# Loads by urgency in a planned four-block kernel: SyncE's time in the orders, first loads on two queues, a bias row behind its buffer

## The chip, the cores and the metric

The kernel runs on one core of a Trainium2 chip. The metric is the device time of one execution in microseconds (us), and the number compared is the median of several runs. A core has five engines, each with its own instruction queue: TensorE (PE; its weight loads are PEld), VectorE (DVE), ScalarE (ACT), GpSimd (POOL) and SyncE (SP), which here only issues transfers from HBM. An engine takes its queue strictly in order: an instruction that waits holds everything behind it.

## What is computed

The reference takes x and a context, both 8 x 128 x 256 in float32, and passes x through four transformer blocks, L0 to L3. All attend to the context.

```
x = L0(x, ctx)   # LN; q from x, k and v from ctx; 16 heads of 16; key mask; LN; MLP 256-1024-256
x = L1(ctx, x)   # keys from ctx and x together; key mask; RMS norm; MLP
x = L2(x, ctx)   # two cross-attentions of 16 heads of 128, each with one learned key and value; MLP
x = L3(x, ctx)   # self-attention with a score mask, cross-attention with a score mask; MLP
```

In L2 the value path has two bias vectors, bv (of the projection) and bias_v (the learned value). The kernel needs their difference as a row of 512 numbers, repeated over all 128 partitions, for each group of four heads.

## The kernel before, in words

**Tiling.** The 8 sequences are split into four threads of two (SIZES), 256 tokens each. `blocks(T)` (L1351) walks a thread through L0 to L3. Threads 0 and 1 start at once; thread 2 starts when thread 0 has left L1 (`front_done`), thread 3 when thread 1 has and thread 0 has left L2 (`wide_done`). Each thread loads its own copy of all weights into eleven slots of 512 KB (NWT), at most four for one thread (NW); `loader(T)` does this. Thread 0 alone makes keys and values of two L2 groups ahead of everything else (AHEAD, 'l10' and 'l11'), so that TensorE has work while L0's chain is short of it.

**The order of the work** is not written out: a planner makes it while the program is built. `Plan` is a simulation of the five engines in Python. Coroutines (`attention`, `mlp`, `group`, `softmax`, ...) ask for an instruction on an engine with `op(eng, f)`; when an engine is free in the simulation, `_choose` takes the request with the smallest urgency (U for the kind of work, plus LATE for the thread and block), runs f, which emits the instruction, and holds the engine for the time that `_weight` gives. `either` lets ScalarE or VectorE take a piece, whichever is free first. If TensorE has nothing to do and `Clock` thinks that its clock is about to be halved, `idle_work` emits a filler, one product of the identity with itself (mm<-ident). The result is one fixed queue for each engine. On the chip only the queues and the semaphores count: where the planner's times are wrong, an instruction stands in the wrong place and its engine waits.

**Loads.** `dma` (L408) asks for SP, then counts 2.8 ns for each KB and 1900 ns to landing. An issue holds SP for 60 ns in the plan (`op`, L341). Nearly all loads ask with urgency 0. The first are x, cols (all per-partition biases, 109 KB) and ctxT (the context's slice) of each thread, from `inputs()`.

**The bias rows.** `value_bias` (L1282) waits for one of two bv slots, loads bv and bb (bias_v) and has GpSimd subtract bb from bv. The pool has two bv buffers but one bb buffer; the plan knows nothing of the latter, so a bb load may be put in SyncE's queue while GpSimd has not yet read the last one. `keys_values` makes the bv tile before it spawns this. The value products (`values`, then `take` on VectorE: vw<-mm,bv) need the row.

**In the profile** every compute instruction has line L329, where `Engine` calls it, and every load L415; so instructions are told apart by tile names: mm, tl and sc are PSUM banks, w a weight, hT a transposed normed input, kb keys, queries or hidden parts, vw values, k, q, v the small attentions' operands, mp their maxima, t scores, pt transposed probabilities, at and attnT attention outputs, xn a normed x, row an output bias.

Of the kernel before, what the change touches and what calls it, by code (L numbers as in the profile page):

```python
# [14 lines left out]
AF = mybir.ActivationFunctionType  # L15
ALU = mybir.AluOpType
AX = mybir.AxisListType

P = 128
# [6 lines left out]
NW, NWT = 4, 11  # L26
# [34 lines left out]

WARM = True
AHEAD = [[(1, 0), (1, 1)], [], [], []]
U = {'take': 0.33, 'taken': -1, 'norm': 0.36, 'mask': 1.35, 'k': 2.41, 'q': 1.92, 'v': 2.5, 'by key': 0.5, 'softmax': 2.4, 'weights': 0.74, 'pairs': 0.3, 'out': 0.94, 'mlp norm': 0.75, 'mlp 1': 3.6, 'mlp 2': 2.28, 'wide norm': -1, 'wide k': 3.49, 'wide q': 4.0, 'wide v': 4.5, 'wide s': 1.19, 'wide': -0.42, 'ahead': 2.48}
LATE = [(2.3, -0.18, 0.84, -0.88, 1.83, -0.17, 2.53, 1.2, 3.66, 1.59), (7.76, 6.61, 5.49, 5.66, 1.7, 0.2, 4.52, 3.1, 7.31, 7.88), (1.86, 2.79, 2.79, -0.1, 2.14, -1, 4.58, 4.78, 5.62, 1.93), (0.03, 1.63, -0.02, 0.92, 0.05, 2.99, -1, 0.16, -1, -1)]


class Event:
# [14 lines left out]
class Plan:  # L83
# [28 lines left out]
    def spawn(self, gen, urgency, after=0):  # L112
        end = Event()
        self.live[id(gen)] = gen
        self._later(self.now + after, (gen, urgency, end), None)
        return end
# [68 lines left out]
        return start + self.weight  # L185

    def run(self):
        self.now = max(self.until.values())
        while self.events or self.asked:
            while self.events and self.events[0][0] <= self.now:  # L190
                _, _, proc, value = heapq.heappop(self.events)
                self._step(proc, value)
            for eng in self.until:
                if self.until[eng] <= self.now:
                    got = self._choose(eng)
                    if not got and eng == "PE" and self.idle_work and (self.events or self.asked):
                        self.weight = 0
                        if self.clock.lazy(self.now) and self.idle_work():
                            self.until[eng] = self._end(eng)
                            self.log.append((eng, self.now, self.until[eng] - self.now, "idle", 2))  # L200
                    if got:
                        _, a, (_, ns, f, lat, table), load = got
                        self.asked.remove(a)
                        self.weight, self.shared, self.wrote, self.count = ns, False, [], 0
                        if load:
                            self.weight += 1295
                            self.table = table[0]
                        value = f()
                        end = self._end(eng)
                        self.until[eng] = end  # L210
                        self.log.append((eng, self.now, end - self.now, f.__qualname__.replace("four_blocks.<locals>.", "").replace("<locals>.", ""), self.count))
                        self._later(end + (self.SEEN[eng] if lat is None else lat), a[2], value)
            at = [self.events[0][0]] if self.events else []
            at += [t for t in self.until.values() if t > self.now]
            if not at:
                break
            self.now = max(self.now, min(at))
        stuck = []
        for g in self.live.values():
            while g:  # L220
                stuck.append(f"{g.gi_code.co_name}:{g.gi_frame.f_lineno}")
                g = g.gi_yieldfrom
        assert not stuck, f"waits without end: {stuck}"


class Clock:


    W, LITTLE, MUCH = 3413, 0.48, 0.87

    def __init__(self):
        self.t, self.busy, self.fast = 0.0, 0.0, False
# [3 lines left out]
    def lazy(self, now):  # L236

        self._go(now, False)
        self.spans = [(a, b) for a, b in self.spans if b > now - self.W]
        return not self.fast or sum(b - max(a, now - self.W) for a, b in self.spans) < 0.55 * self.W  # L240

    def _go(self, to, busy):
        while self.t < to:
# [19 lines left out]
def _weight(eng, name, args, kw):  # L263

    aps = [x for x in (*args, *kw.values()) if isinstance(x, bass.AP)]
    sizes = [x.free_size() for x in aps]
    n = max(sizes)
    by_part = sum(m == 1 for m in sizes[1:]) if n > 2 else max(0, len(aps) - 2) if name == "tensor_scalar" else 0
    on_sbuf = all(x.space == bass.MemoryType.SB for x in aps)
    if eng == "PE":  # L270
# [9 lines left out]
    if eng == "ACT":  # L280
        if "accum_out" in kw:
            return 385, False
        if name == "copy":
            return 61 + 0.824 * n, False
        return 127 + 0.805 * n + (40 if isinstance(kw.get("bias"), bass.AP) else 0) + (
            90 if isinstance(kw.get("scale"), bass.AP) else 0), False
    if eng == "DVE":
        if name == "reciprocal":
            return 65 + 6.25 * n, False
        if name in ("bn_stats", "bn_aggr"):  # L290
            return (325 if name == "bn_stats" else 99), False
        if n <= 8:
            return 68, False
        if name in ("tensor_scalar", "tensor_copy") and on_sbuf:
            return 75 + 0.8 * n + 55 * by_part, True
        two = name in ("tensor_tensor", "scalar_tensor_tensor") and sum(
            x.space == bass.MemoryType.SB and x.free_size() > 1 for x in aps[1:]) == 2
        return 72 + 1.03 * n + 55 * by_part, two
# [40 lines left out]


def op(eng, f, lat=None, table=None):  # L341
    return ((eng, 60 if eng == "SP" else 0, f, lat, table),)


EXP = ("exp",)
# [5 lines left out]
def four_blocks(ctx: ExitStack, tc: tile.TileContext, a: dict, out: bass.AP):  # L351
# [33 lines left out]
    pt_small, pt_wide, tm_slots = Slots(2), Slots(2), Slots(2)  # L385
    kb_slots, v_slots = Slots(20), Slots(4)
    attn_lock, x1_slots = Slots(2), Slots(2)
    row_slots, bv_slots, w_slots = Slots(2), Slots(2), Slots(NWT)

    def kb():  # L390
        return new(act, [P, 2 * P], "kb", bufs=20)
# [13 lines left out]
        at = COL_AT[name] + k  # L405
        return cols[:, at : at + n]

    def dma(f, kb_):  # L408

        yield op("SP", f)  # L410
        plan.dma_until = max(plan.dma_until, plan.now) + kb_ * 2.8
        yield plan.dma_until - plan.now + 1900

    def load(dst, src, kb_):
        return dma(lambda: nc.sync.dma_start(out=dst, in_=src), kb_)  # L415

    ident = new(const, [P, P], "ident")
    make_identity(tc.nc, ident)
# [86 lines left out]
    def loader(T):  # L505
        names = list(weight_list())
        first = {f"l{i}{hg}{x}" for i, hg in AHEAD[T.h] for x in "kv"}
        ahead = [x for x in names if x[0] in first]
        names = [x for x in names if x[0] not in first]
        for name, shape, pieces in names[:2] + ahead + names[2:]:  # L510
            yield (T.w_slots, 1)
            yield (w_slots, 1)
            t = T.w[name] = new(wpool, shape, "w", bufs=NWT)
            ends = [spawn(load(at(t), src, int(np.prod(shape)) // 256 // len(pieces)), 0) for at, src in pieces]
            T.w_in.setdefault(name, Event())
            spawn(all_then(ends, T.w_in[name]), 0)

# [32 lines left out]
    def asks(r):  # L550
        yield r
# [613 lines left out]
    def keys_values(T, i, hg, step_back):  # L1165

        n = f"l{i}{hg}"
        ks, vs = [], []
        bv = new(wpool, [P, 512], "bv", bufs=2)
        bv_in = spawn(value_bias(bv, i, hg), U["mask"] + step_back)  # L1170
        nb, nt = T.nb, T.nt
        v_in = [Event() for _ in range(nb)]

# [22 lines left out]
        def values():  # L1196
# [3 lines left out]
            for b in range(nb):  # L1200
# [9 lines left out]
                        )  # L1210

                def take(p, b=b, t=t):
                    yield op("DVE", lambda: nc.vector.tensor_tensor(t, p, bv, ALU.add))
                    plan.set(v_in[b])
                yield from product([f], take)
            drop(T)
# [62 lines left out]
            yield e  # L1279
        drop(T)  # L1280

    def value_bias(bv, i, hg):  # L1282
        s = slice(hg * 512, (hg + 1) * 512)
        yield (bv_slots, 1)
        bb = new(wpool, [P, 512], "bb", bufs=1)
        e = spawn(load(bv, a[f"L2_bv{i}"][:, s].partition_broadcast(P), 256), 0)
        yield from load(bb, a[f"L2_bias_v{i}"][:, s].partition_broadcast(P), 256)
        yield e
        yield op("POOL", lambda: nc.gpsimd.tensor_tensor(bv, bv, bb, ALU.subtract))

    def after_scores(T, i, hg, b, s, vs, v_in, n):
        t = new(act, [P, 516], "t", bufs=NT_).rearrange("p (h k) -> p h k", h=4)
# [111 lines left out]
    def inputs():  # L1404
        for T in threads:
            h = T.h
            if h == 0:
                first = new(const, [P, 1], "first")
                spawn(asks(op("ACT", lambda: nc.scalar.activation(first, ident[:, :1], AF.Exp), None, EXP)), 0)
            e = spawn(load(T.x, a["x"][T.batches].rearrange("b p d -> p b d"), 128 * T.nb), 0)  # L1410
            spawn(all_then([e], T.ready), 0)
            if h == 0:
                e = spawn(load(cols, a["cols"], 140), 0)
                spawn(all_then([e], cols_in), 0)
            e = spawn(load(T.ctx, a["ctxT"].rearrange("(c p) t -> p c t", p=P)[:, :, T.tokens], 128 * T.nb), 0)
            spawn(all_then([e], ctx_in[h]), 0)
            spawn(blocks(T), 0)
            yield 2000 if h == 0 else 8000
    plan.idle_work = idle_work if WARM else None
    spawn(inputs(), 0)  # L1420
    spawn(learned_keys(), 5.0)
# [43 lines left out]
```

## Time and profile before

| what | value |
|---|---|
| runs | 1213.44, 1214.82, 1214.67 us; median 1214.67 |
| profiled execution | 1218.14 us, its span 1216.3 us, granted TensorE clock 0.986 |
| instructions | 21992 |
| TensorE weight loads (PEld) busy | 950.5 us (78%) |
| ACT_TABLE_LOAD (the switch between exp and gelu) | 42, 53.9 us |
| DMA moved | 145.59 MB, 120 GB/s over the span |
| last chain by engine | PE 74%, DVE 16%, ACT 4%, DMA 3% |

The span goes from the first to the last instruction. "Busy" is the time in which at least one instruction of an engine runs. A timeline row has the start, the length in us, the engine, the instruction, out<-in, the number of instructions, and in brackets the idle time before it with what ended it. A window's row has the stretch, its length, for each engine the busy time and the number of instructions, and at the end the granted clock (1.00 is full speed), the DMA engines' busy share and GB/s. A group's row ends with the idle time ahead of its instructions.

### The profile page before, as it was taken

To read this page: it belongs to the slowest core of one execution; us is meant where nothing else is said; L and a number is where in the kernel's file an instruction comes from. 1 tells how busy PE (TensorE), PEld (TensorE's weight loads), DVE (VectorE), ACT (ScalarE), POOL (GpSimd) and SP (SyncE) were. 2 spreads that over 40 slices of the span, in tenths; PEclk is the share of its full clock that TensorE was granted. 3 is DMA by queue.
4 is the path that set the end of the run, shared out by engine and by line. 5 is a ranking of instruction groups with operands and counts; after the bars stand their busy time and mean duration, and the time that the engine had idled before them with its cause. 6 is when DMAs were issued, how large, how long until landed. Compare 5 with 4: busy or idle time off the path is not lost.

```text
span 1216.3 us, 21992 instructions
## 1 busy us (share of the span) xinstructions
PE 1163.1 (96%) x8352; PEld 950.5 (78%) x8352; DVE 747.2 (61%) x1927; ACT 560.3 (46%) x1428; POOL 340.2 (28%) x393
## 2 busy tenths in 40 slices
PE   7998999999999999999999999999999999998988
PEld 6686778888787788887778887887878888876767
DVE  4665846764666384784776725554545475868872
ACT  3345344453443243457365423332424363686962
POOL 3011201122112032044243201121221272566870
PEclk9899998999999999999999999999999999999999
DMA  7623232335325534252532455344454535332120
GB/s 224 198 62 122 71 100 50 105 109 156 104 90 176 172 120 139 89 164 65 150 96 84 126 168 164 102 156 139 148 163 135 150 118 157 107 98 84 38 73 18
DMA packets 107321, 145.59 MB, mean 120 GB/s; under 512 B 6736, under 2 KB 66256, under 8 KB 107216
## 3 DMA queue, kind: packets, MB, share of 16 engines
q1 hardware_dynamic: 107216, 144.18, 38.9%
q8 instruction: 66, 1.08, 0.4%
q14 instruction: 39, 0.32, 0.1%
HBM read 143.11 MB, written 1.05 MB: 119 GB/s over the span
## 4 chain that ended last, share of the span: by engine, by line
PE 74%; DVE 16%; ACT 4%; DMA 3%; issue 1%; POOL 1%; SPq 0%; ACTq 0%; POOLq 0%; DVEq 0%
PE mm L329 54%; PE tl L329 15%; PE sc L329 5%; DVE t L329 2%; DVE tm L329 2%; DVE rz L329 1%; DVE mx L329 1%; DVE mp L329 1%; ACT t L329 1%; DVE q L329 1%; ACT q L329 1%; DVE rv L329 1%; DVE sm L329 1%; POOL t L329 1%; DVE st L329 1%
## 5 line engine op out<-in xcount | busy, mean ns | idle before, releaser
L329 PE MATMUL mm<-hT,w 128*128 128x256 f32 x1216 | 285.7, 383 | 5.5 <-ACT hT L329 1.9
L329 PEld LDWEIGHTS mm<-hT,w 128*128 128x128 f32 x1216 | 224.5, 191 | 42.6 <-ACT kb L329 3.6
L329 POOL TENSOR_TENSOR t<-t,sm 128x512 f32<-128x512 f32 x128 | 131.9, 1042 | 342.7 <-DVE sm L329 265.6
L329 PE MATMUL mm<-ctxT,w 128*128 128x256 f32 x608 | 146.2, 386 | 8.0 <-DVE kb L329 3.6
L329 PE MATMUL mm<-w,ctxT 128*128 128x512 f32 (+1 forms) x352 | 144.6, 542 | 3.9 <-ACT q L329 2.9
L329 POOL TENSOR_TENSOR x<-x,row 128x512 f32<-128x512 f32 x40 | 50.8, 1270 | 318.1 <-ACT xn L329 117.2
L329 PEld LDWEIGHTS mm<-ctxT,w 128*128 128x128 f32 x608 | 112.8, 192 | 25.9 <-issue 4.8
L329 DVE TENSOR_TENSOR x<-mm,x 128x256 f32<-128x256 f32 (+1 forms) x96 | 48.7, 508 | 122.3 <-PE mm L329 121.6
L329 PE MATMUL mm<-w,at 128*128 128x256 f32 x512 | 121.2, 381 | 1.1 <-DVE vw L329 1.1
L329 PE MATMUL mm<-w,kb 128*128 128x256 f32 x512 | 116.5, 380 | 0.0
L329 PEld LDWEIGHTS mm<-w,at 128*128 128x128 f32 x512 | 95.0, 190 | 17.6 <-issue 3.2
L329 PEld LDWEIGHTS mm<-w,kb 128*128 128x128 f32 x512 | 95.8, 190 | 14.6 <-issue 1.3
L329 ACT ACTIVATE t<-t,mn 128x128 f32<-128x128 f32 x256 | 99.0, 393 | 6.0 <-DVE mn L329 5.1
L329 PEld LDWEIGHTS mm<-w,ctxT 128*128 128x128 f32 x352 | 64.5, 193 | 43.5 <-issue 33.1
L329 POOL TENSOR_TENSOR t<-t,mask 128x512 f32<-128x512 f32 x64 | 80.0, 1275 | 13.8 <-DVE t L329 10.8
L329 PE MATMUL tl<-ident,t 128*128 128x128 f32 x512 | 75.6, 277 | 6.2 <-POOL t L329 2.1
L329 ACT ACTIVATE kb<-mm,cols 128x256 f32<-128x256 f32 x128 | 53.0, 472 | 58.9 <-PE mm L329 58.6
L329 PEld LDWEIGHTS tl<-ident,t 128*128 128x128 f32 x512 | 60.0, 142 | 24.6 <-issue 8.9
L329 ACT ACTIVATE kb<-mm,sb 128x256 f32<-128x256 f32 x72 | 32.7, 471 | 91.4 <-PE mm L329 90.6
L329 ACT ACTIVATE at<-tl,cols 128x128 f32<-128x128 f32 x188 | 53.4, 369 | 44.2 <-PE tl L329 44.1
L329 ACT ACTIVATE t<-t 128x516 f32<-128x516 f32 x64 | 40.4, 633 | 72.1 <-DVE t L329 71.9
L329 PEld LDWEIGHTS tl<-kb,kb 128*128 128x128 f32 x512 | 64.3, 192 | 10.3 <-issue 7.7
(118 smaller groups left out, 1800.5 us busy)
## 6 DMA issues: line engine op xcount, KB each, us to landing
w<-in_L_wk SPq DMA_DIRECT2D x32, 512.0 KB, 4.0
w<-in_L_wv SPq DMA_DIRECT2D x32, 512.0 KB, 4.2
w<-in_L_wq SPq DMA_DIRECT2D x32, 512.0 KB, 4.0
w<-in_L_wo SPq DMA_DIRECT2D x32, 512.0 KB, 4.0
bv<-in_L_bv SPq DMA_DIRECT2D x32, 256.0 KB, 4.5
bb<-in_L_bias_v SPq DMA_DIRECT2D x32, 256.0 KB, 5.3
w<-in_L_mlp_w SPq DMA_DIRECT2D x16, 512.0 KB, 4.2
w<-in_L_w_fc SPq DMA_DIRECT2D x16, 512.0 KB, 4.0
```

What stands on the lines that cost most here:

```text
L329: return f(*args, **kw)
```

## The change

Six things are done.

1. `dma` takes the engine as an argument; loads marked `early` may be issued by SP or by ACT, whichever the plan finds free. Early are x and ctxT of threads 0 and 1, cols, and thread 0's L0 attention weights.
2. Loads have urgencies: -3 for x, ctxT and cols, U["load"] (-0.39) for weights, 2 less for the early ones, U["load"] plus the group's own lateness for the bias rows. The activation that loads the exp table first gets urgency 9; thread 1 starts its loads 4000 ns after thread 0 and not 2000.
3. In the plan an issue costs 480 ns of SP (and of ACT), and landing 2300 ns instead of 1900.
4. `value_bias` makes the bv tile and issues its load only when a bv slot is free, and takes a slot for bb (`bb_slots`, one) that is given back after GpSimd's subtraction.
5. Costs in `_weight` are adjusted (an activation from SBUF with 256 elements, small tensor_scalar, bn_stats, bn_aggr), the engines' start times in the plan are set, and `Clock`'s thresholds change.
6. U and LATE have new numbers, so the whole order is drawn anew.

In the order as built, SyncE's first loads are ctxT, k_w, q_w, mask, wk, wv, row, bv, bv, then thread 1's ctxT, mask and weights; the first bb is its 18th load and the second its 25th. ScalarE issues x, cols, v_w, cproj_w, then the table load, the `first` activation and x of thread 1. Fillers go from 64 to 47, table loads from 42 to 50, and at<-tl,cols activations of 128 columns on ScalarE from 188 to 224 (nine groups of four that were one VectorE instruction of 512 columns each).

```diff
-U = {..., 'ahead': 2.48}
+U = {..., 'ahead': 4.34, 'load': -0.39}
...
-        self.now = max(self.until.values())
+        self.until.update({"DVE": 1900, "POOL": 1500, "PE": 1500})
...
-    W, LITTLE, MUCH = 3413, 0.48, 0.87
+    W, LITTLE, MUCH = 3413, 0.41, 0.84
...
+    if name == "dma_start":
+        return 480, False
...
-    return ((eng, 60 if eng == "SP" else 0, f, lat, table),)
+    return ((eng, 480 if eng == "SP" else 0, f, lat, table),)
...
-    def dma(f, kb_):
-        yield op("SP", f)
+    def dma(f, kb_, early):
+        yield op("SP", lambda: f(nc.sync)) + (op("ACT", lambda: f(nc.scalar)) if early else ())
         plan.dma_until = max(plan.dma_until, plan.now) + kb_ * 2.8
-        yield plan.dma_until - plan.now + 1900
+        yield plan.dma_until - plan.now + 2300
...
-            ends = [spawn(load(at(t), src, int(np.prod(shape)) // 256 // len(pieces)), 0) for at, src in pieces]
+            early = T.h == 0 and name.startswith("a0")
+            ends = [spawn(load(at(t), src, int(np.prod(shape)) // 256 // len(pieces), early), U["load"] - 2 * early)
+                    for at, src in pieces]
...
-    def value_bias(bv, i, hg):
+    def value_bias(to, i, hg, step_back):
         s = slice(hg * 512, (hg + 1) * 512)
         yield (bv_slots, 1)
+        bv = new(wpool, [P, 512], "bv", bufs=2)
+        to.append(bv)
+        e = spawn(load(bv, a[f"L2_bv{i}"][:, s].partition_broadcast(P), 256), U["load"] + step_back)
+        yield (bb_slots, 1)
         bb = new(wpool, [P, 512], "bb", bufs=1)
-        e = spawn(load(bv, a[f"L2_bv{i}"][:, s].partition_broadcast(P), 256), 0)
-        yield from load(bb, a[f"L2_bias_v{i}"][:, s].partition_broadcast(P), 256)
+        yield spawn(load(bb, a[f"L2_bias_v{i}"][:, s].partition_broadcast(P), 256), U["load"] + step_back)
         yield e
         yield op("POOL", lambda: nc.gpsimd.tensor_tensor(bv, bv, bb, ALU.subtract))
+        plan.put(bb_slots)
...
+            rows = (load(T.x, a["x"][T.batches].rearrange("b p d -> p b d"), 128 * T.nb, early),
+                    load(T.ctx, a["ctxT"].rearrange("(c p) t -> p c t", p=P)[:, :, T.tokens], 128 * T.nb, early))
+            for f, then in zip(rows, (T.ready, ctx_in[h])):
+                spawn(all_then([spawn(f, -3)], then), 0)
```

More of the change, by code (lines that the diff above doesn't have):

```diff
@@ L63 @@
 AHEAD = [[(1, 0), (1, 1)], [], [], []]
-U = {'take': 0.33, 'taken': -1, 'norm': 0.36, 'mask': 1.35, 'k': 2.41, 'q': 1.92, 'v': 2.5, 'by key': 0.5, 'softmax': 2.4, 'weights': 0.74, 'pairs': 0.3, 'out': 0.94, 'mlp norm': 0.75, 'mlp 1': 3.6, 'mlp 2': 2.28, 'wide norm': -1, 'wide k': 3.49, 'wide q': 4.0, 'wide v': 4.5, 'wide s': 1.19, 'wide': -0.42, 'ahead': 2.48}
-LATE = [(2.3, -0.18, 0.84, -0.88, 1.83, -0.17, 2.53, 1.2, 3.66, 1.59), (7.76, 6.61, 5.49, 5.66, 1.7, 0.2, 4.52, 3.1, 7.31, 7.88), (1.86, 2.79, 2.79, -0.1, 2.14, -1, 4.58, 4.78, 5.62, 1.93), (0.03, 1.63, -0.02, 0.92, 0.05, 2.99, -1, 0.16, -1, -1)]
+U = {'take': -0.44, 'taken': -1, 'norm': -0.47, 'mask': 0.26, 'k': 2.41, 'q': 1.79, 'v': 2.5, 'by key': 0.5, 'softmax': 2.46, 'weights': 1.63, 'pairs': 0.75, 'out': 1.79, 'mlp norm': 0.75, 'mlp 1': 4.29, 'mlp 2': 1.92, 'wide norm': -1, 'wide k': 3.49, 'wide q': 4.0, 'wide v': 4.43, 'wide s': 1.19, 'wide': -0.3, 'ahead': 4.34, 'load': -0.39}
+LATE = [(1.69, 2.1, 2.22, -0.57, 1.75, 0.04, 2.53, 1.2, 4.53, 1.81), (12.77, 7.95, 10.47, 7.4, 1.7, -1, 8.48, 3.14, 7.46, 6.32), (3.27, 2.62, 3.89, 0.6, 2.14, -1, 4.58, 4.56, 5.62, 0.26), (0.03, 1.69, 0.31, 1.11, 0.24, 3.18, -0.81, -0.64, -0.7, 1.05)]
 class Event:
@@ L239, in lazy @@
         self.spans = [(a, b) for a, b in self.spans if b > now - self.W]
-        return not self.fast or sum(b - max(a, now - self.W) for a, b in self.spans) < 0.55 * self.W
+        return not self.fast or sum(b - max(a, now - self.W) for a, b in self.spans) < 0.52 * self.W
     def _go(self, to, busy):
@@ L284, in _weight @@
             return 61 + 0.824 * n, False
-        return 127 + 0.805 * n + (40 if isinstance(kw.get("bias"), bass.AP) else 0) + (
+        return 127 + 0.805 * n + (35 if on_sbuf and n == 256 else 0) + (40 if isinstance(kw.get("bias"), bass.AP) else 0) + (
             90 if isinstance(kw.get("scale"), bass.AP) else 0), False
     if eng == "DVE":
+        if name == "tensor_scalar" and n == 4 and len(aps) == 2 and len(args) > 5:
+            return 145, False
         if name == "reciprocal":
@@ L290, in _weight @@
         if name in ("bn_stats", "bn_aggr"):
-            return (325 if name == "bn_stats" else 99), False
+            return (330 if name == "bn_stats" else 150), False
         if n <= 8:
@@ L387, in four_blocks @@
     attn_lock, x1_slots = Slots(2), Slots(2)
-    row_slots, bv_slots, w_slots = Slots(2), Slots(2), Slots(NWT)
+    row_slots, bv_slots, bb_slots, w_slots = Slots(2), Slots(2), Slots(1), Slots(NWT)
     def kb():
@@ L406, in col, with load @@
         return cols[:, at : at + n]
-    def dma(f, kb_):
-        yield op("SP", f)
+    def dma(f, kb_, early):
+        yield op("SP", lambda: f(nc.sync)) + (op("ACT", lambda: f(nc.scalar)) if early else ())
         plan.dma_until = max(plan.dma_until, plan.now) + kb_ * 2.8
-        yield plan.dma_until - plan.now + 1900
-    def load(dst, src, kb_):
-        return dma(lambda: nc.sync.dma_start(out=dst, in_=src), kb_)
+        yield plan.dma_until - plan.now + 2300
+    def load(dst, src, kb_, early=False):
+        return dma(lambda eng: eng.dma_start(out=dst, in_=src), kb_, early)
     ident = new(const, [P, P], "ident")
@@ L1168, in keys_values @@
         ks, vs = [], []
-        bv = new(wpool, [P, 512], "bv", bufs=2)
-        bv_in = spawn(value_bias(bv, i, hg), U["mask"] + step_back)
+        bv = []
+        bv_in = spawn(value_bias(bv, i, hg, step_back), U["mask"] + step_back)
         nb, nt = T.nb, T.nt
@@ L1212, in take @@
                 def take(p, b=b, t=t):
-                    yield op("DVE", lambda: nc.vector.tensor_tensor(t, p, bv, ALU.add))
+                    yield op("DVE", lambda: nc.vector.tensor_tensor(t, p, bv[0], ALU.add))
                     plan.set(v_in[b])
@@ L1406, in inputs @@
             h = T.h
+            early = h < 2
+            rows = (load(T.x, a["x"][T.batches].rearrange("b p d -> p b d"), 128 * T.nb, early),
+                    load(T.ctx, a["ctxT"].rearrange("(c p) t -> p c t", p=P)[:, :, T.tokens], 128 * T.nb, early))
+            for f, then in zip(rows, (T.ready, ctx_in[h])):
+                spawn(all_then([spawn(f, -3)], then), 0)
             if h == 0:
+                spawn(all_then([spawn(load(cols, a["cols"], 140, True), -3)], cols_in), 0)
                 first = new(const, [P, 1], "first")
[L1409 to L1416, printed above, removed]
+                spawn(asks(op("ACT", lambda: nc.scalar.activation(first, ident[:, :1], AF.Exp), None, EXP)), 9)
             spawn(blocks(T), 0)
-            yield 2000 if h == 0 else 8000
+            yield 4000 if h == 0 else 8000
     plan.idle_work = idle_work if WARM else None
```

## The prediction

> **What bounds the kernel now.** I read in this order: the page's busy shares, the windows by stage, the waits of SyncE's queue, the timelines at the start and at 586 to 600 us. The profiled execution took 1218.14 us, 1.84 more than its span of 1216.3; the median of the runs is 1214.67, so 3.47 under it. I sum against 1218.14 and take the sum off the median.
>
> ```profile
> PE 1163.1 (96%) x8352; PEld 950.5 (78%) x8352; DVE 747.2 (61%) x1927; ACT 560.3 (46%) x1428; POOL 340.2 (28%) x393
> L329 PE MATMUL mm<-ident 128*128 128x128 f32 x128 | 26.5, 352 | 5.3 <-DVE v L329 2.0 <-POOL ident masks.py:199 1.4 <-DVE vw L329 1.2
> ```
>
> TensorE is the bound. Its useful work isn't changed, so only what it loses can be won: 1216.3 - 1163.1 = 53.2 us idle, 26.5 us of fillers (64 products of the identity, 0.41 us each, counted as busy), and a halved clock (granted 0.50 in the window 30 to 33 us), (1 - 0.986) x 1216.3 = 17 us. The windows (PE busy first, then the clock and DMA columns at the end) tell where:
>
> ```profile
> 0.00:60.00 60.00, 50.79 (x398) 38.52 (x402) 35.30 (x107) 21.53 (x42) 12.62 (x29) 0.90 0.66 214
> 60.00:240.00 180.00, 168.70 (x1610) 137.21 (x1603) 115.66 (x301) 81.82 (x141) 25.66 (x41) 0.96 0.28 84
> 240.00:540.00 300.00, 295.40 (x1938) 242.86 (x1937) 185.73 (x482) 123.75 (x248) 59.25 (x74) 1.00 0.44 133
> 540.00:660.00 120.00, 113.47 (x897) 90.59 (x900) 81.00 (x193) 70.88 (x215) 52.26 (x56) 0.99 0.35 104
> 1080.00:1216.30 136.30, 121.68 (x1052) 99.23 (x1044) 90.23 (x242) 89.13 (x324) 77.30 (x76) 0.99 0.20 61
> ```
>
> The first 60 us lose 9.2 idle, some 6 to the clock, and most of 9 us of fillers; 60 to 240, where only two threads run, 11.3 idle; the middle little, but for 6.5 at 540 to 660; the end 14.6. The start, from the timeline:
>
> ```profile
> 2.63 0.94 SPq L415 DMA_DIRECT2D bv<-in_L_bv  x2
> 3.62 0.43 SPq L415 DMA_DIRECT2D w<-in_L_k_w  x1
> 10.32 9.05 SPq L415 DMA_DIRECT2D bb<-in_L_bias_v  x2
> 11.21 3.54 PE L329 MATMUL mm<-ctxT,w 128*128 128x256 f32 x8 [1.29 <-DMA w<-in_L_k_w]
> 20.88 0.47 SPq L415 DMA_DIRECT2D w<-in_L_k_w  x1
> 26.80 2.60 PE L329 MATMUL mm<-ctxT,w 128*128 128x256 f32 x8 [3.43 <-DVE kb L329]
> ```
>
> The first true product waits until 11.21 for a weight issued behind two bias rows that nobody needs yet. SyncE then stands 9 us at the second bb row, whose one buffer GpSimd has not yet read; behind it stand all loads of the second thread, and TensorE runs dry at 23.4.
>
> **Part 1, first loads.** As built, SyncE issues ctxT, k_w, q_w, mask; ScalarE x, cols, v_w, cproj_w. Bytes up to the first product: x, ctxT and k_w 256 KB each, cols 109: 877 KB. In the trace x is used at 5.08 with 288 KB moved. The remaining 589 KB at 360 GB/s (the rate of the window 23.4 to 36) take 1.7 us: start at 6.8, gain 4.4. Here the Trainium skill speaks against the change: "DMA: Bandwidth & Descriptors", section "Issuing engines are not separate DMA queues", says that loads from several engines share the same DMA engines and only issue time is saved. That would be 4 x 0.47 = 1.9 us. I keep 4.4: the gain is not the second queue but the 512 KB of bias rows that move behind k_w, and the rows show k_w waiting its turn. The cost: on ScalarE the load of the second x waits for an early load's end (estimate 9 us) with the first xn behind it, which ran at 8.22; hT is 1 us later. The product of the keys (2 us) hides some; TensorE waits for xn about 1.5.
>
> **Part 2, the bias row.** The first bb row is now the 18th load on SyncE, the second the 25th, and bv_slots and bb_slots are taken before the load is issued. Only the start has two groups at once; later bb loads are at most 3.4 us held by GpSimd in the SyncE waits, so nothing more is won there. The second bb row lands near 30, after GpSimd's first subtraction; behind it on SyncE stand wv and the MLP's weights, wanted from 40 on, and GpSimd's second subtraction: hidden by some 8 us. Up to the second thread's k_w there are now 4141 KB, from 288 KB at 5.1: 3853 KB at 360 GB/s is 11 us, and the two bv rows, which are slow, add 2: it lands at 18, wanted at 20 to 22. So 3.43 + 0.83 us of waits go, and the halved clock they brought (0.73 over 12.6 us, 3.4). What is late next: the second thread's wide key weight, which by the same sum lands at 29 where TensorE wants it at 28, and VectorE, which must still do the mask's small steps, 2.35 us of maxima and 1.66 of keys before the scores.
>
> Sum of 1 and 2: 4.4 + 4.3 + 3.4 = 12.1, less 1.5 for xn, 1 to 2 for the wide weight, 2 for VectorE: **7**, ends 3 and 11. The stall at 55 to 59 us (1.24 and 2.8 of filler, behind VectorE's vw and maxima) has the same work in front of it in the new order and stays.
>
> **Part 3, SyncE's time in the orders** (480 ns for an issue instead of 60, 2300 ns to landing instead of 1900). Nothing runs faster; instructions that wait for a load stand later in their queue; the new U, LATE and small costs move orders in the same way. One place shows it:
>
> ```profile
> 584.71 0.54 SPq L415 DMA_DIRECT2D mask<-in_mask_x  x1
> 592.62 1.15 DVE L329 TENSOR_SCALAR mask<-mask 128x256 f32<-128x256 f32 x1 [2.48 <-DMA mask<-in_mask_x]
> 596.91 2.68 PE L329 MATMUL mm<-w,ctxT 128*128 128x256 f32 x8 [2.90 <-ACT q L329]
> 832.86 1.32 PE L329 MATMUL mm<-ctxT,w 128*128 128x256 f32 x5 [1.42 <-DMA w<-in_L_wk]
> ```
>
> A mask landed 7.9 us after its issue behind a batch of weights; VectorE stood 2.48 us with the q behind it, TensorE 2.90, and the clock fell (0.93 over 25 us, 1.75). With 1.42 at 832.86 and 1.12 behind a bias row at 637 that is 7.2 us. But all orders are drawn anew, and the new one has places of its own: I take **4**, ends -5 (new stalls) and 10.
>
> **Part 4, fillers, tables, shares.** The order has 47 fillers, 17 fewer. Five stand ahead of the first product (counted above); the rest are idle time that isn't filled, worth 0 to 5 us; I take 1. Table loads go from 42 to 50. The row is
>
> ```profile
> 544.53 1.28 ACT L329 ACT_TABLE_LOAD   x1
> 545.83 0.40 ACT L329 ACTIVATE t<-t,mn 128x128 f32<-128x128 f32 x1
> ```
>
> so 1.30 us each, 8 more are 10.4 us of ScalarE. "ScalarE: Activation LUTs", section "What ACT_TABLE_LOAD costs", puts a drain beside it, 2.66 us a switch, 21 us in all; here the next instruction starts 0.02 us after the load, so the row decides. At 540 to 565 us there are eight such loads, ScalarE is busy 24.58 of 25 us, and TensorE lost 1.85: a price of 0.23 a load on the path, so 8 cost **2**; the end is 10.4 if none is hidden. Nine more at-groups go to ScalarE (9 x 4 x 0.37 = 13 us; VectorE loses 9 x 0.69). They lie beside matmuls; with ScalarE at 46% I cost them at nothing; without that cover 7 us.
>
> **Sum.** -7 - 4 - 1 + 2 = -10: 1208 profiled, 1204.7 for the median. I say 1204.
>
> **Rivals.**
> A: the new order pays in full: part 3 at 10 and half the 11.3 idle at 60 to 240 gone, since both threads' loads come early: -7 - 10 - 5 + 2 = -20, **1195**. For it: most stalls there are on one late step. Against: at 60 to 240 the waits are ScalarE's and VectorE's (pt, mp, xn, v), not loads. Chance 0.25.
> B: the start is won and given back: the two threads meet the same chains (maxima, exponentials, MLP) and stand there longer, as at 55 us, and the change hardly does what it says: -2 from parts 1 and 2, -2 from part 3, -1 + 2: -3, **1212**. Chance 0.16.
> C: slower, by ScalarE's tables. The order has 15 table loads in the 120 us of useful work that had 7 in the same stretch (thread 0's softmax beside other threads' MLPs). If ScalarE is full there, as at 540 to 565, each switch is paid: 10.4, with a halved clock behind two gaps, 3.4, and part 3 turns to +3: -7 + 10.4 + 3.4 + 3 = +10, **1224**. It decides once ScalarE is busy over 97% for some 50 us on end and TensorE waits for kb. Against it: ScalarE's 46%, and the price of 0.23 that the trace shows. Chance 0.10.
>
> **Numbers.** Forecast 0.46, A 0.25, B 0.16, C 0.10, other 0.03. Measurement tells 0.2% (2.4 us) from no change: faster is under 1212.2. Forecast and A are faster nearly whole, B in part: 0.81. Same 0.08 (from B), slower 0.11 (C and some of the rest). Range: down past A's center, up past B's: **1193 to 1213**; it leaves out some of A and all of C.
>
> **What would show it.** First true product at 6.5 to 7.5 us; no SyncE wait of over 3 us in the first 20; the second thread's keys without a wait, near 21; the first 60 us with under 6 us idle and a clock of 0.95. At 540 to 660 less than 4 us idle if part 3 holds. Fifty table loads, ScalarE near 590 us busy. Wrong if the idle time of 60 to 240 us or 400 to 600 us grows by more than the start wins.

## The result, and the profile after

The changed kernel takes **1199.05 us** (median of 4 runs, 1197.24 to 1201.26) against 1214.06 for the kernel before: ratio 0.9879, 95% interval 0.9857 to 0.9901, or 14.7 us less (0.0121 times 1214.06). Its profiled execution took 1198.46 us, with a span of 1196.7 and a granted clock of 0.996. The two traces lie 19.6 us apart, 4.9 more than that, because the trace of before comes from one of its slower executions (1218.14); what is read from the two traces side by side is too long by up to this much.

The engines' busy time first, then ScalarE's table loads (from the groups by line):

```profile
PE 1145.7 (96%) x8318; PEld 937.0 (78%) x8318; DVE 751.2 (63%) x1943; ACT 574.1 (48%) x1448; POOL 339.1 (28%) x392
L333 ACT ACT_TABLE_LOAD x50 | 64.2, 1283 | 15.0 <-PE sc L333 8.4 <-DVE mn L333 3.0 <-issue 2.8
```

TensorE's idle time hardly moved: 1196.7 - 1145.7 = 51.0 us, 53.2 before. What fell is its busy time, 1163.1 to 1145.7, for the same useful work. Where nothing else runs beside them, fillers went from 24.6 to 14.8 us; the other 7.7 us are the same useful products in less time, since the clock's loss (the part that wasn't granted times its stretch) went from 17.3 to 5.1 us, in part under fillers and idle time. The same stretches as before, PE busy second, then the other engines, and the clock third from the end:

```profile
0.00:60.00 60.00, 50.89 (x480) 38.87 (x480) 43.87 (x131) 22.99 (x41) 12.44 (x30) 0.94 0.69 225
60.00:240.00 180.00, 166.61 (x1559) 135.67 (x1548) 121.92 (x330) 83.97 (x148) 28.84 (x44) 0.99 0.28 89
240.00:540.00 300.00, 293.71 (x2021) 241.27 (x2019) 187.04 (x476) 143.63 (x324) 75.28 (x93) 1.00 0.41 128
540.00:660.00 120.00, 117.77 (x959) 96.44 (x960) 78.90 (x208) 62.43 (x151) 32.57 (x32) 1.00 0.36 111
1080.00:1196.70 116.70, 102.24 (x866) 83.72 (x864) 76.96 (x218) 72.66 (x258) 64.13 (x62) 1.00 0.18 55
```

The first 60 us hold 448 records of useful products (480 less 32 of fillers) for 352 (398 less 46), so they do more in the time. The start from the timeline:

```profile
6.51 1.96 PE L333 MATMUL mm<-ctxT,w 128*128 128x256 f32 x8
13.05 1.97 PE L333 MATMUL mm<-hT,w 128*128 128x256 f32 x8 [1.05 <-ACT k L333]
15.87 0.47 SPq L420 DMA_DIRECT2D bb<-in_L_bias_v  x1
20.44 1.89 PE L333 MATMUL mm<-ctxT,w 128*128 128x256 f32 x8
23.20 0.34 SPq L420 DMA_DIRECT2D bb<-in_L_bias_v  x1
26.95 1.89 PE L333 MATMUL mm<-ctxT,w 128*128 128x256 f32 x8
49.02 2.09 PE L333 MATMUL sc<-k,q 32*128 32x128 f32 x32 [2.46 <-DVE mp L333]
```

The first true product runs at 6.51 (11.21 before), the second thread's keys at 20.44 and its wide keys at 26.95, both without a wait. The stall behind VectorE's maxima is still there, at 46 to 49. If matching instructions of the two traces are laid side by side, the lead is 9.0 us at 62 us, 9.1 at 135, 10.3 at 165, then 14.6 at 177: 4.4 us, three tenths of it, come from one place that the prediction passed over. The fillers there, before:

```profile
180.84 7.10 PE L329 MATMUL mm<-ident 128*128 128x128 f32 x18 [1.97 <-DVE v L329]
183.87 0.34 DVE L329 SCALAR_TENSOR_TENSOR tm<-tl,odd,tm 128x128 f32<-128x128 f32 x1
187.73 1.06 PE L329 MATMUL tl<-ident,xn 128*128 128x128 f32 x4
```

Nine fillers in a row (18 records) first wait for a PSUM bank that VectorE's v gives back, then run at a granted clock of 0.56 over the stretch (0.50 from 181.65 on), 0.79 us each. The transposes behind them need xn (ready at 181.1) and a tl bank (free when tm ends, 184.21), so the fillers hold real work from about 184.3 to 187.73. The changed order has three fillers at that place.

### The profile page after: what moved, and what is told of

Same layout as the page of the kernel before. It is cut to its first block, busy times and chain, and to the rows that moved or that the text cites. A ratio compares the mean times of both kernels' runs of the same rounds, so it can differ in the third digit from the quotient of the medians.

```text
span 1196.7 us, 21922 instructions
## 1 busy us (share of the span) xinstructions
PE 1145.7 (96%) x8318; PEld 937.0 (78%) x8318; DVE 751.2 (63%) x1943; ACT 574.1 (48%) x1448; POOL 339.1 (28%) x392
## 3 DMA queue, kind: packets, MB, share of 16 engines
HBM read 143.11 MB, written 1.05 MB: 120 GB/s over the span
## 4 chain that ended last, share of the span: by engine, by line
PE 78%; DVE 13%; ACT 5%; issue 1%; POOL 1%; DMA 0%; ACTq 0%; POOLq 0%; DVEq 0%
PE mm L333 57%; PE tl L333 17%; PE sc L333 5%; DVE t L333 2%; DVE mp L333 1%; DVE rz L333 1%; ACT t L333 1%; ACT pt L333 1%; DVE mn L333 1%; ACT q L333 1%; POOL t L333 1%; DVE ry L333 1%; DVE q L333 1%; ACT L333 1%; DVE rv L333 1%
## 5 line engine op out<-in xcount | busy, mean ns | idle before, releaser
L333 ACT ACTIVATE t<-t,mn 128x128 f32<-128x128 f32 x256 | 99.1, 390 | 11.6 <-DVE mn L333 10.3
L333 ACT ACTIVATE at<-tl,cols 128x128 f32<-128x128 f32 x224 | 64.0, 369 | 62.2 <-PE tl L333 61.9
L333 POOL TENSOR_TENSOR bv<-bv,bb 128x512 f32<-128x512 f32 x32 | 40.7, 1271 | 178.6 <-DMA bb<-in_L_bias_v 153.7
L333 POOL TENSOR_TENSOR t<-t,mask 128x512 f32<-128x512 f32 x64 | 79.8, 1273 | 26.3 <-DVE t L333 22.4
L333 DVE TENSOR_TENSOR vw<-mm,bv 128x512 f32<-128x512 f32 x64 | 43.7, 684 | 46.8 <-PE mm L333 46.6
```

Of the source, the lines that this page charges most:

```text
L333: return f(*args, **kw)
```

## The experiments

Theory 1: parts 1 and 2 make the start, the lost filler run adds some 3 to 5 us, and the rest of the new order is worth little. Theory 2: the re-drawn order is what counts. In the first four runs all engines' orders were held as in the kernel before (the plan counts the same times; only what is emitted differs), so each edit stands alone. Us are the ratio's distance from 1 times the median of before in that comparison.

**The bias row alone** (the second bb row goes into thread 3's x, which is loaded later):

```diff
+    rows = []
...
-        bb = new(wpool, [P, 512], "bb", bufs=1)
+        rows.append(i)
...
+        bb = threads[3].x.rearrange("p b d -> p (b d)") if len(rows) == 2 else new(wpool, [P, 512], "bb", bufs=1)
```

> The kernel before, every engine's order as it was; only the second bb row goes into a buffer that is free at the start (thread 3's x, which is loaded later), so that SyncE does not stand at it until GpSimd has read the first row, and the second thread's first loads follow at once. Theory 1 (start and fillers: the start is worth the 9 us that the two traces show at 50 us, and a run of nine fillers near 180 us another 5): the second thread's key weight lands near 18 instead of 26.3, its keys start without the waits of 3.43 and 0.83, the stall near 56 stays; about 1209 (1207 to 1211). Theory 2 (the re-drawn order: only an order drawn with the right times keeps a gain; in the old order the later waits give it back): within 2.4 of before, 1212 to 1215.

Measured: 1207.92 against 1213.36, ratio 0.9943 (0.9928 to 0.9957), 6.9 us less.

```profile
13.86 0.37 SPq L415 DMA_DIRECT2D w<-in_L_k_w  x1
21.24 1.99 PE L329 MATMUL mm<-ctxT,w 128*128 128x256 f32 x8 [0.27 <-DVE kb L329]
24.66 1.17 PE L329 MATMUL sc<-k,q 32*128 32x128 f32 x32 [1.43 <-DVE ry L329]
```

The second thread's key weight was issued at 13.86 instead of 20.88 and landed at 19.27, not 26.3. Its keys, at 21.24, no longer waited for it: 0.27 us of idle time is left of 3.43. The wait before the scores didn't go with it; it is 1.43 us instead of 0.83. Theory 1, and a little faster than its figure of 1209.

**The first loads alone** (thirteen loads gathered and issued as context, key weight, x, cols, query weight, mask, ... with the two bv rows last, all on SyncE):

```diff
+    kept = []
...
+    def held(f):
+        kept.append(f)
+        if len(kept) == 13:
+            for j in (3, 6, 1, 2, 8, 0, 7, 9, 10, 11, 12, 4, 5):
+                kept[j]()
+        elif len(kept) > 13:
+            f()
...
-        yield op("SP", f)
+        yield op("SP", lambda: held(f))
```

> The kernel before, every other engine's order as it was; only the first thirteen loads are issued in another order on SyncE: context, key weight, x, cols, query weight, mask, value weight, output weight, wk, wv, rows and then the two bv rows. The first product on real data starts near 7.5 instead of 11.2. Theory 1 says that this alone is lost at the next wait, since the second bb row still holds SyncE until about 19 and the second thread's key weight still lands near 26: 1213 to 1214.5. The sum of the prediction (part 1 pays by itself) says about 3 to 4 less: 1210 to 1211. Theory 2 (order): no change.

Measured: 1212.10, ratio 0.9988 (0.9976 to 1.0), 1.5 us less, an interval that ends at no change. The first product came at 10.58, not 7.5. My expectation overlooked TensorE's order: before the product stand 17 fillers and the first transposes, and those waited for xn until 9.71. Only the new order puts the product first. The second thread's key weight still landed at 24.34, and its keys, at 24.86, still had 2.08 us of idle time before them. So the loads alone are worth little; the figure lies between those of theory 1 and of the prediction's sum.

**Eight fillers near 180 us left out:**

```diff
+    fills = [0]
...
+                fills[0] += 1
+                if fills[0] - 1 in range(40, 48):
+                    count[0] += 1
+                    plan.weight += 225
+                    plan.count += 2
+                else:
+                    nc.tensor.matmul(bank(tag)[:, :P], lhsT=ident, rhs=ident, start=True, stop=True)
```

> The kernel before, order as it was; eight of the fillers (the products of the identity with itself, which are no part of the computation) are left out: those that stand in TensorE's queue near 180 us, in a run of nine ahead of the transposes of a normalised x that has long been ready. Theory 1: the transposes start at about 182 instead of 187.7, and 4 to 6 us of it reach the end: about 1209 (1208 to 1211). Theory 2: the run stands in time that is idle anyway, or the clock drops further without it and gives the time back: 1213 to 1215, or above.

Measured: 1210.54, ratio 0.9973 (0.9961 to 0.9985), 3.3 us less. In its timeline the transposes follow tm directly:

```profile
178.59 0.49 PE L329 MATMUL mm<-ident 128*128 128x128 f32 x2 [1.96 <-DVE v L329]
181.62 0.34 DVE L329 SCALAR_TENSOR_TENSOR tm<-tl,odd,tm 128x128 f32<-128x128 f32 x1
182.11 1.09 PE L329 MATMUL tl<-ident,xn 128*128 128x128 f32 x4 [3.03 <-ACT k L329]
```

From v's release to the transposes it is 3.5 us instead of 6.9, a gain of 3.4, and 3.3 arrive at the end. The row puts the wait down to ScalarE's k; the bank, freed by tm 0.15 us earlier, fits better, since the transposes don't read k. This is why the gain is not the whole 6.3 us (8 x 0.79) that eight fillers took.

**The three together, old order:**

> The three edits together in the old order: the second bb row in a free buffer, the first loads re-ordered on SyncE, and the eight fillers near 180 us left out (they are no part of the computation). Theory 1: the start is then as early as in the changed kernel (lead near 9 at 60 us) and the filler run is gone: 1199 to 1202, the changed kernel's time, without its new order. Theory 2: without the new order most of it is given back at waits further on: 1205 or more.

Measured: 1203.20, ratio 0.9913 (0.9886 to 0.9940), 10.6 us less; the three alone add to 11.7. It lies between the two theories. So most of a gain like the change's can be had without the new order, but perhaps not all. (The changed kernel has fewer fillers at that place by its new order, not by an edit of their own.)

**The changed kernel again,** with three variants beside it:

> The changed kernel once more, as the measure for the three runs beside it, and against the three edits in the old order (ratio 0.9913). Theory 1 (start 8 to 9, filler run 3, little else): its ratio comes down to 0.990 to 0.992, the same as that of the three edits. Theory 2 (the re-drawn order is worth something of its own, 3 to 4): it stays at 0.986 to 0.989.

Measured: 1199.46 against 1211.62, ratio 0.9901 (0.9874 to 0.9927), 12.0 us less. The intervals of 0.9879, 0.9901 and 0.9913 overlap, so the medians don't tell whether the new order adds anything of its own.

**One queue** (in `dma`, the order of everything else held):

```diff
-        yield op("SP", lambda: f(nc.sync)) + (op("ACT", lambda: f(nc.scalar)) if early else ())
+        def as_on_act():
+            f(nc.sync)
+            plan.weight += 480
+            plan.count += 1
+        yield op("SP", lambda: f(nc.sync)) + (op("ACT", as_on_act) if early else ())
```

> The changed kernel, every engine's order as it is; only the five loads that ScalarE issues (x, the columns, value weight and output weight of the first thread, x of the second) are issued by SyncE, in the place where they stand in time. The first key weight's issue comes about 1.0 us later, wk about 2. Theory 1 (the order of the loads makes the start, the second queue only saves issuing time): the first product near 7.5 instead of 6.5, the end 1 to 2 later, 0.9885 to 0.9895 of before. Rival (the second queue is the start): 4 or more later, above 0.991.

Measured: 1200.90, ratio 0.9903 (0.9882 to 0.9925), the same as the changed kernel beside it. In its trace the price isn't where I put it:

```profile
6.75 1.97 PE L333 MATMUL mm<-ctxT,w 128*128 128x256 f32 x8 [0.50 <-DMA w<-in_L_k_w]
15.07 3.35 PE L333 MATMUL mm<-hT,w 128*128 128x256 f32 x8 [4.19 <-ACT k L333]
```

The first product is only 0.24 us later. The mask, eighth in the one queue, lands at 11.90 instead of 7.63, the first scores' k waits for it, and the query product is 2.0 us later. In this trace 2.5 us of it are still there at 100 us; the medians differ by 1.4 us, inside the 1 to 2 that I expected, which the intervals don't separate from nothing. The rival of 4 or more is out as a median.

**The bias rows back in front of the second thread's loads:**

```diff
...
+            def both(eng):
+                eng.dma_start(out=bv, in_=bv_row)
+                eng.dma_start(out=bb, in_=bb_row)
+            e = spawn(dma(both, 256, False), U["load"] + step_back)
...
```

> The changed kernel, every other engine's order as it is; only the first two bb rows are issued directly behind the two bv rows again, ahead of the second thread's loads, into the one buffer, so that SyncE stands at the second one until GpSimd has read the first. Theory 1: GpSimd can read it near 17, the second thread's key weight lands near 21 to 23 instead of 16.1 and is wanted at 20.4: 1 to 4 us slower than the changed kernel, 0.989 to 0.991 of before. Rival (the buffer rule is worth in the new order what it is in the old one, 6.9): 0.993 or more. Second rival (the re-drawn order, not the row, makes the gain): no change.

Measured: 1203.70, ratio 0.9927 (0.9904 to 0.9950); by the medians 4.2 us above the changed kernel beside it, though the two intervals overlap. That is past theory 1's ratio of 0.989 to 0.991 and just short of the rival's 0.993; the interval holds both.

```profile
15.26 0.33 SPq L1303 DMA_DIRECT2D bb<-in_L_bias_v  x1
21.87 1.96 PE L333 MATMUL mm<-ctxT,w 128*128 128x256 f32 x8 [1.22 <-DMA w<-in_L_k_w]
31.51 3.26 PE L333 MATMUL mm<-ctxT,w 128*128 128x256 f32 x8 [3.66 <-DMA w<-in_L_wk]
```

SyncE passes the second row at 15.26, 3.8 us earlier than in the kernel before. GpSimd reads the first row at 13.96 instead of 17.75: in its queue an addition of the output-bias row (x<-x,row) stands in front of the subtraction, and that row landed at 12.43 instead of 16.35, since the two bv rows no longer go ahead of it. The keys wait 1.22, and then the wide keys, which I hadn't counted here, 3.66: 4.9 of the 5.4 us by which this trace is behind the changed kernel's at 100 us.

**Fillers placed otherwise in the changed kernel** (seven at 46 us, two fewer at 172):

```diff
+    fills = [0]
...
+                n, fills[0] = fills[0], fills[0] + 1
+                if n not in (29, 30):
+                    t = bank(tag)
+                    for _ in range(7 if n == 12 else 1):
+                        plan.weight = plan.count = 0
+                        nc.tensor.matmul(t[:, :P], lhsT=ident, rhs=ident, start=True, stop=True)
+                plan.weight, plan.count = 225, 2
```

> The changed kernel with its fillers (products of the identity with itself, no part of the computation) placed otherwise: seven instead of one in the stall at 46 to 49 us, where the granted clock fell to 0.58 to 0.67 until 55, and two fewer at 172 us, where they run into the time at which the transposes could start. Theory: the clock stays at 1.0 there and the transposes start 0.5 us earlier: 1 to 3 us faster than the changed kernel, 0.985 to 0.987 of before. Rival: the clock's fall in that stall is a matter of chance in one execution, and nothing is gained: within 1 us of the changed kernel.

Measured: 1197.97, ratio 0.9878 (0.9853 to 0.9903); the median is 1.5 us under the changed kernel's, as forecast in size, but not separated from nothing. The window from 45 to 56 us shows what the fillers do to the clock, first the changed kernel's repeat, then this one (clock third from the end):

```profile
45.00:56.00 11.00, 7.32 (x62) 5.80 (x58) 8.15 (x11) 0.40 (x1) 0.00 (x0) 0.69 0.17 49
```

```profile
45.00:56.00 11.00, 8.14 (x104) 6.80 (x100) 10.10 (x21) 1.31 (x2) 0.00 (x0) 1.00 0.41 100
```

With one filler in the stall both traces of the changed kernel fall to 0.69; with seven, 1.00, and this trace leads the first by 2.1 us from 56 us on, by 2.7 from 173 us (the two fewer there) and by 3.35 at the end. The fall is not chance in one execution: the runs with one queue, with the row back and with the two nudged urgencies below have the same stall with one filler, and each shows the clock halved for 3.4 or 6.8 us in it or just behind it. With seven there is one trace. It is the best version I ran by its median, and I don't claim more.

**Is it the counting of SyncE's time, or a draw?** Four kernels with orders drawn anew. The yardstick is TensorE's idle time and fillers from 240 us to 115 us before the end.

```diff
# SyncE at 60 ns again, in the changed kernel
-    return ((eng, 480 if eng == "SP" else 0, f, lat, table),)
+    return ((eng, 60 if eng == "SP" else 0, f, lat, table),)
# q nudged, in the changed kernel
-'q': 1.79
+'q': 1.92
# norm nudged, in the changed kernel
-'norm': -0.47
+'norm': -0.3
# the kernel before, SyncE's time alone
-    return ((eng, 60 if eng == "SP" else 0, f, lat, table),)
+    return ((eng, 480 if eng == "SP" else 0, f, lat, table),)
-        yield plan.dma_until - plan.now + 1900
+        yield plan.dma_until - plan.now + 2300
```

> The changed kernel, but the plan counts a step of SyncE at 60 ns again instead of 480 (everything else of the change stays, the urgencies too, so the orders are drawn anew). Told by TensorE's idle time with the fillers between 240 us and 115 us before the end, 20.3 before and 14.4 in the changed kernel. Theory A (it is the counting of SyncE's time that takes waits out of the middle): 18 to 21 there, the time 3 to 6 above the changed kernel. Theory B (the orders are a tuned draw, in which any re-drawing loses): as bad as the nudged orders beside it. Theory C (neither): 14 to 16.

> The changed kernel with one urgency nudged (q 1.79 to 1.92, its value before): the first 350 rows of TensorE's order stay, the rest is drawn anew with the right time for SyncE. Theory A: the middle keeps its idle time, 14 to 17 us, and the time stays within 2 of the changed kernel. Theory B (a tuned draw): 18 or more, and 3 to 8 slower.

> The changed kernel with another urgency nudged (norm -0.47 to -0.3): the first 428 rows of TensorE's order stay. Theory A: 14 to 17 us idle in the middle, within 2 of the changed kernel. Theory B: 18 or more, and 3 to 8 slower.

> The kernel before with two numbers of the plan alone changed, a step of SyncE counted at 480 ns instead of 60 and a transfer's latency at 2300 instead of 1900; old urgencies, old loads, old buffer rule. Theory A: the middle's idle time falls from 20.3 to 15 to 17, though the start stays as late as before: 1207 to 1211. Theory B: the old urgencies were fitted to the old numbers, so the order gets worse: 20 or more idle in the middle and 1213 to 1222.

| kernel | median, us | ratio (interval) | idle + fillers in the middle, us | in the last 115 us |
|---|---|---|---|---|
| before | 1212.04 | 1 | 20.3 + 0.0 | 12.4 + 4.2 |
| changed | see above | 0.9879 (0.9857 to 0.9901) | 14.4 + 0.9 | 14.1 + 2.6 |
| three edits, old order | see above | 0.9913 (0.9886 to 0.9940) | 18.9 + 0.0 | 13.1 + 4.2 |
| SyncE at 60 | 1244.25 | 1.0262 (1.0233 to 1.0291) | 22.9 + 1.2 | 17.0 + 19.7 |
| q nudged | 1235.32 | 1.0188 (1.0159 to 1.0216) | 23.7 + 0.7 | 16.1 + 20.5 |
| norm nudged | 1211.07 | 0.9987 (0.9973 to 1.0001) | 19.9 + 4.2 | 15.3 + 2.4 |
| before, SyncE at 480 | 1216.60 | 1.0032 (1.0019 to 1.0045) | 18.6 + 1.1 | 16.9 + 8.0 |

All four fall on the side of theory B (a tuned draw), and the two nudges further than it said: 3 to 8 us above the changed kernel were expected, some 36 and 12 came. Only the last kernel misses B's sign, with 18.6 us of idle time in the middle where it had 20 or more. The windows of the changed kernel and of the one with q nudged, middle and end:

```profile
240.00:1081.70 841.70, 827.25 (x5440) 679.84 (x5438) 510.10 (x1272) 395.53 (x1004) 234.89 (x259) 1.00 0.42 130
1081.70:1196.70 115.00, 100.90 (x856) 82.61 (x854) 75.29 (x213) 71.58 (x256) 62.98 (x60) 1.00 0.18 56
```

```profile
240.00:1115.60 875.60, 851.92 (x5698) 700.27 (x5697) 530.36 (x1350) 417.76 (x1070) 257.33 (x281) 1.00 0.42 128
1115.60:1230.60 115.00, 98.94 (x681) 81.12 (x679) 48.63 (x129) 47.52 (x168) 40.45 (x38) 0.93 0.11 35
```

With q nudged TensorE's order is the changed kernel's up to 333 us (2504 of its 8318 products), loads and bias row too, and yet the median is some 36 us worse. VectorE's busy time in the last 115 us falls from 75 to 49 and the transfers from 56 to 35 GB/s: less work is left for the end, TensorE fills it with 20 us of fillers and the clock falls to 0.93. Counting SyncE's time in the old kernel, with the old urgencies, loses 3.9 us. So it can't be said that counting it wins: as far as these four tell, each order is a draw, and the change's is a good one for the numbers it came with. The kernel with SyncE at 60 can't be read as the price of not counting, for the same reason.

One stretch looks like a gain of the counting: in the old kernel with SyncE at 480, TensorE's idle time from 540 to 660 us is 2.0, not 6.5.

```profile
540.00:660.00 120.00, 118.01 (x975) 95.29 (x974) 87.33 (x215) 58.79 (x157) 37.48 (x37) 1.00 0.35 113
```

This kernel loses it again in the last 115 us (24.9 us of idle time and fillers for 16.6). And with SyncE at 60 in the changed kernel the same stretch has 3.6, so it doesn't tell counting from a new order.

## Why the prediction was right, and where not

- **The total.** 1204 forecast, 1199.05 measured, on the forecast side and inside the range; the first measurement says -14.7 and the repeat -12.0 where the sum said -10. The direction and the place of the start were worked out; that the total came so near is luck in part, since part 3's 4 us have no shown cause. Most of the 4.7 us by which the sum falls short of the first measurement are the fillers (2.3 too little) and the table loads (2 charged, nothing seen).
- **Parts 1 and 2: 7, measured 7 to 8.** The two edits alone give 6.9 and 1.5, and the three together less the fillers 10.6 - 3.3 = 7.3. In the traces the lead at 60 us is 9, but some 2 us of that is the trace of before: the run without the eight fillers, the same up to 170 us, leads it by 2.2 at 65 us. The 3.4 for the halved clock held: both traces have 6.8 us at half clock (from 28.05 before, from 25.48 without the fillers), and none of the three with loads moved has any between 24 and 36 us.
- **Part 1 by itself.** First product 6.8 forecast, 6.51 measured. The working named the wrong agent in part: the loads' order moves little as long as TensorE's old order stands in front of it (1.5 us for the 4.4 of the sum). The cost, 1.5 for xn, was 0.92 before the transposes, and 1.05 more for k. Against the second queue I was right to lean on the order: the rule of the Trainium skill, "DMA: Bandwidth & Descriptors", section "Issuing engines are not separate DMA queues", that only issue time is saved, fits the first product in the run with one queue: it comes 0.24 us later, and 4.5 of the 4.7 us up to it stay. The mask, issued 2.0 us later there, landed 4.3 later, so its place among the loads counted beside the issue time.
- **Part 2.** The key weight was to land at 18 and landed at 16.14; the keys at 20.44 without a wait, and SyncE's longest wait in the first 20 us is 1.94, as said. The term "what is late next", 1 to 2 us for the wide key weight, didn't come: it landed at 25.0, not 29, and was wanted at 26.95. With the row put back it did come, at 3.66. SyncE's stand at the second bb row was 8.4 us; the 9.05 of the row that I read takes in both issues.
- **First 60 us: under 6 us idle was wrong, 9.1;** the clock of 0.95 was 0.94. I said that the stall at 55 stays, and it does; that the new order puts one filler there instead of six, so that it is idle time and brings the clock down to 0.69, I had not looked at. By the run with seven fillers it gives back 2.1 us of the start.
- **Part 3: 4, the size seen, the reason not shown.** From 240 us to 115 us before the end the idle time fell from 20.3 to 14.4, and 540 to 660 us to 2.2, under the 4 that was to show it. But the stall of 2.90 at 596.91, the one place that I showed for it, is 0.79 with the three edits in the old order, without any counting: there the mask landed 6.1 us after its issue, not 7.9, and VectorE's 2.48 are gone (why it landed sooner, I didn't test). With only the bias row moved it is 1.01. Counting alone clears 540 to 660 us and loses in total; the kernel with q nudged has 1.2 idle there and is slower by 1.9%. So the size holds by the trace, and that counting made it isn't shown. Nor was the lower end of -5 wide enough: the order with q nudged costs some 36 us beside the changed one, 23 beside before.
- **Part 4, fillers: 1, measured 3.3.** This is the term that was mis-sized. I wrote that fillers other than the first five "are idle time that isn't filled". At 181 to 188 us they were queued work at half clock in front of transposes that were ready, as the eight left out show.
- **Part 4, tables: 2, nothing seen.** There are 50 loads, as said, of 1.283 us; but the last 115 us have 16.7 us of idle time and fillers after and 16.6 before, and ScalarE is busy 574 us, not 590. No experiment took the loads away, so their price isn't measured.
- **Rivals.** A's figure (1195) is a little nearer than the forecast's, but its reason, both threads' loads early in 60 to 240 us, fell: that stretch's idle time rose from 11.3 to 13.4. What the stretch gained came from fillers (10.7 to 4.7 us) and from the clock (0.96 to 0.99). B's giving back was real, small, and at the place that it named. C's outcome, a clearly slower kernel, came in two of the re-drawn orders (SyncE at 60 and q nudged), by thin ends; its sign, ScalarE busy over 97% of some 50 us, came in neither (76% and 75% at most) nor in the changed kernel (86%).

What stays open is what the new order is worth by itself: 14.7 or 12.0 less 10.6 is 1 to 4 us, within the intervals.

## What to carry to other kernels

A filler that a planner puts into an in-order queue is work as soon as the instruction behind it is ready (3.4 us here): look in the trace for runs of them in front of an instruction whose operands are ready, and for stalls that have too few, and move them. When a change draws an order anew, hold the order and make each edit alone before any part of the time is put down to a reason; a nudge of one unrelated number shows how wide the draws lie. A gain at a load is worth what the next wait leaves of it (1.5 of 4.4 us here), so two edits at the start are tested together and apart.

## What the hardware showed that I had not expected

- With the same instructions in the same order the granted clock fell at different places: from 10 to 15 us it was 0.66 in the profiled run of before and 1.00 in that of the kernel without the eight fillers, alike up to 170 us. The second led by 2.65 us at 15 us, lost all of it at the wait for the second thread's key weight at 27, and led by 2.2 at 65: lengths of one trace's start are uncertain by some 2 us.
- The kernel before ran from 1209.57 to 1218.99 in 54 runs, wider than its first three (1213.44 to 1214.82) let one think; its profiled execution, at 1218.14, was near the top.
- A filler took 0.79 us at half clock in the run at 181 us, against 0.41 on average; in all six traces with one filler before the stall of 2.46 us near 50 us the clock was halved there or just behind it for 3.4 or 6.8 us, and in the one with six more fillers it stayed at 1.00.
